# Scores and exponentials of layer 0 in two tiles of two heads; one TensorE allowance split into two; the norms behind layer 1 as threads of their own

## The chip, the core and the metric

The kernel is one program on one core of a Trainium2 chip. TensorE multiplies matrices from SBUF into PSUM, VectorE and ScalarE do elementwise work and evictions, GpSimd does some elementwise work and issues software DMAs, SyncE issues the other DMAs. All arithmetic is float32. The metric is the device time of one execution in microseconds (us); the kernel before is given by the median of 13 runs, and one further execution was profiled.

## The reference

The input x is 8 images of 256 channels by 32 x 32 positions. Two layers follow each other:

```python
# layer 0
x = x + L0_conv(_gn(x))          # 8 heads of 32 channels, 1024 queries,
                                 # 1426 keys: k and v maps pooled to 32^2, 16^2, 11^2, 5^2,
                                 # each with a 3x3 depthwise convolution and a layer norm
    # attn = softmax(q k^T * 32**-0.5);  out = attn v;  a 32x32 mix of each head;  projection
# layer 1, tokens t = [8, 1024, 256]
t = t + attention(_ln_t(t))      # one head of 256, softmax over 1024 keys, divided by its sum
t = t + ffn(_ln_t(t))            # 8 experts, three 256x256 matmuls each, relu between them;
                                 # the experts' outputs are weighed by a gate that is made
                                 # from the mean of all 8 images' normed tokens
```

So the feed-forward part needs the second norm (`_ln_t` behind layer 1's attention) of every image before its gate is known.

## The kernel before

`attention()` holds layer 0 and layer 1's attention of all images, `experts()` the feed-forward part. A third part, `layer0_general` and `layer1_general`, is run only for inputs for which the fast softmax could overflow; it is not run here and has no place in the profile.

**The main loop.** Layer 0's attention is 8 images x 2 groups of 4 heads x 2 halves of the queries (512 each) x 12 chunks of 128 keys (the last one has 18) = 384 steps. In step i, `scores` (L1434) issues four matmuls, one for each head, each on its own 32 rows of the array, into one PSUM tile `sc` of four banks, and ScalarE takes all of it through one exponential of 2048 columns into an SBUF tile `pt` (6 buffers). `sc` has one buffer, so the scores of step i+1 wait for the exponential of step i. Behind the scores of step i, TensorE has `values` of step i-1 (four matmuls, each on its own 32 columns of the array, into `pv`). Every second step, GpSimd issues a DMA that adds one `pt` tile onto the one before it (1 MB, written back to SBUF); VectorE adds such pairs up in `sums`, whose total is the softmax's denominator.

**What lies between the steps.** All other work is written as Python generators ("threads") with a rank: `unit` 0 (the sums and the division), `project` 1 (projection and residual, result to DRAM as `t1`), `keys_and_values` and `pool_levels` 2, `first_diagonals` 3, `prepare` 4 (the next image's group norm, maps and queries), `outputs` and the weights' set-up 5, `layer1` 6, `convolve` 7 (VectorE's convolution), `gates` 7. A thread yields what it needs next: an engine, the tiles that must be ready, a PSUM tag. `Flow` (L654) keeps a planned clock for each engine from fixed costs (0.00169 us a column for a TensorE matmul, a quarter and 0.05 us for one on 32 rows or columns), and `step()` resumes the first thread, in order of rank, that `runnable()` admits. The order of instructions on every engine is therefore fixed when the program is built.

**The allowance.** A TensorE piece is admitted while `credit` is above zero, or while the planned TensorE clock lies more than 0.5 us before the time at which `sc` will be free, less 0.5 us; its inputs have to be ready 1.5 us before that time in any case. Each step adds `PACE` = 3.2 us to `credit`, up to 1.5 times that; each piece takes its planned cost from it. All ranks share this one number.

**Layer 1.** `layer1` makes an image's scores in 16 pieces (tiles `p1`, 6 buffers), and stays at most six pieces ahead of `outputs`. `outputs` takes a quarter of an image's queries at a time: the sum of the exponentials, the product with v, the division into an SBUF tile `o`, bias and residual (`res`, read from `t1`), the store to `t2`, then `scale_tokens` (transposes on TensorE, statistics on VectorE, a power and a diagonal on GpSimd, a matmul that spreads the scale, a multiplication) and the store to `hn`. Only then does it take the next quarter. `o` and `res` have one buffer each.

**Behind the loop.** `experts()` runs the first two matmul stages of the experts (stage one with plain products, 4 x 512 columns) while layer 1 of the last image and the gate are still being finished (`PACE2` = 8 us of allowance a step). Once the gate is known, it goes on with seven products of 256 columns in place of eight.

Of the kernel before, what the change touches and what calls it, by code (L numbers as in the profile page):

```python
# [10 lines left out]
AF = mybir.ActivationFunctionType  # L11
ALU = mybir.AluOpType
# [4 lines left out]
P = 128  # L17
C = 256
HW = 1024
HEADS = 8  # L20
DH = 32
# [4 lines left out]
NE = 8  # L26
SCALE0 = DH ** -0.5
SCALE1 = C ** -0.5
PACE = 3.2
CAP = 1.5  # L30
NEVER = 1e9
MARGIN = 1.5
AHEAD = {"DVE": 4.0, "ACT": 2.0, "POOL": 4.0, "SP": 10.0}
# [2 lines left out]
PACE2 = 8.0  # L36
# [617 lines left out]
class Flow:  # L654
# [18 lines left out]
    def __init__(self, tc, kit):  # L673
        nc = tc.nc
        self.tc, self.kit = tc, kit
        self.now = dict.fromkeys(("PE", "DVE", "ACT", "POOL", "SP"), 0.0)
        self.last = {}
        self.ready, self.read, self.writer, self.reader, self.slots, self.open = {}, {}, {}, {}, {}, set()
        self.pe = self.Engine(self, "PE", nc.tensor)
        self.ve = self.Engine(self, "DVE", nc.vector)  # L680
        self.act = self.Engine(self, "ACT", nc.scalar)
        self.pool = self.Engine(self, "POOL", nc.gpsimd)
        self.sp = self.Engine(self, "SP", nc.sync)
        self.threads = []
        self.cut = {}
        self.also = {}
        self.credit, self.port = 0.0, 0.0

    def tile(self, pool, shape, tag, bufs=1):
        t = self.kit.tile(pool, shape, tag, bufs=bufs)  # L690
# [111 lines left out]
            self.threads.insert(at, thread)  # L802
        return thread

    def runnable(self, need):
        engine, tiles, tag = need
        if engine is None:
            return tiles()
        at = max([self.ready.get(n, 0.0) for t in tiles for n in self.keys(t)], default=0.0)
        pe = self.now["PE"]  # L810
        if engine == "PE":

            until = max(pe, self.free("sc") - 0.5)
            slot = self.free(tag) if tag is not None else 0.0
            return (
                not self.closed
                and (self.credit > 0 or pe < until - 0.5)
                and at + MARGIN <= until
                and slot <= until
            )  # L820

        now = self.now[engine]
        return now <= pe + AHEAD[engine] if at <= now + 0.3 else at <= pe + NEAR[engine]

    def resume(self, thread):
        pe = self.now["PE"]
        thread[1] = next(thread[0], None)
        if thread[1] is None:
            self.threads = [t for t in self.threads if t is not thread]
        self.credit -= self.now["PE"] - pe  # L830

    def step(self, pace=None):


        self.closed = pace is None
        if pace is not None:
            self.credit = min(self.credit + pace, CAP * pace)
        while True:
            thread = next((t for t in self.threads if self.runnable(t[1])), None)
            if thread is None:  # L840
                return
            self.resume(thread)

    def finish(self, done):

        while not done():
            self.credit, self.closed = 1.0, False
# [14 lines left out]
def attention(tc, kit, f, outer, ended, nb, consts, x, t1, t2, hn, bounds, vecs, q_t, kv_t, proj_t, gqk_t, wqk, wqkv, vecs1, w1_d, w1c, gate_d, wrc, vecs2, bnvec):  # L862
# [6 lines left out]
    with ExitStack() as ctx:  # L869
        l1, shared = outer  # L870
        wp = ctx.enter_context(tc.tile_pool(name="w0", bufs=1))
        work = ctx.enter_context(tc.tile_pool(name="work0", bufs=1))
        psum = ctx.enter_context(tc.tile_pool(name="psum0", bufs=1, space=PSUM))

        def T(pool, shape, tag, bufs=1):
            return f.tile(pool, shape, tag, bufs=bufs)
# [34 lines left out]
        heads = T(l1, [P, P + DH], "o")  # L911
        nc.scalar.dma_start(heads, consts[:, K_HEAD:K_SEL])
        head = heads[:, :P]

# [115 lines left out]
        ks, qs, vts = {}, {}, {}  # L1030
# [402 lines left out]

        def scores(b, c, sl, kc):  # L1434
            k0, w = KEY_CHUNKS[kc]
            t = T(psum, [P, 4, 512], "sc")
            for j in range(4):
                r = slice(DH * j, DH * j + DH)
                f.pe.matmul(t[:w, j, :], lhsT=ks[b, c][r, k0 : k0 + w], rhs=qs[b, c][r, sl], start=True, stop=True)
            pt = T(work, [P, 4, 512], "pt", bufs=6)  # L1440
            f.act.activation(pt[:w], t[:w], AF.Exp, scale=SCALE0)
            return pt

        def values(b, c, kc, pt, pv):
# [106 lines left out]
        projected, taken, written, probabilities = [0], [0], [0], []  # L1551
# [55 lines left out]
        def outputs():  # L1607

            for i in range(4 * nb):
                yield until(lambda: len(probabilities) > i)  # L1610
                b, q, p1, v = probabilities[i]
                res = T(l1, [P, 2, C], "res")
                f.sp.dma_start(res, t1[b][:, :, q])
                s = T(l1, [P, 2, C], "s")
                yield ve(*p1[:2])
# [15 lines left out]
                ps = small()  # L1631
                for m in range(2):
                    for kc in range(8):
                        if kc % 4 == 0 and (m or kc):
# [3 lines left out]
                            lhsT=v[:, kc, m * P : (m + 1) * P],  # L1638
                            rhs=p1[kc // 2][:, kc % 2, :],
                            start=kc == 0,  # L1640
                            stop=kc == 7,
                        )
                taken[0] += 1
                yield ve(ps, rec)
                o = T(l1, [P, 2, C], "o")
                f.ve.tensor_tensor(
                    o, ps.rearrange("p (m q) -> p m q", m=2), rec[:, None, :].to_broadcast([P, 2, C]), ALU.mult
                )
                for m in range(2):
                    f.ve.scalar_tensor_tensor(o[:, m, :], o[:, m, :], gb[:, m : m + 1], res[:, m, :], ALU.add, ALU.add)  # L1650
                f.sp.dma_start(t2[b][:, :, q], o)
                yield from scale_tokens(o, C)
                f.sp.dma_start(hn[b][:, :, q], o)
                written[0] += 1
                ended[0] = written[0] // 4

        def centred(cm, src, width, dst):

# [14 lines left out]
        def weights1():  # L1673
# [36 lines left out]
            ps = small()  # L1710
            for m in range(2):
                for k in range(2):
                    f.pe.matmul(
                        ps[:, m : m + 1],
                        lhsT=raw[:, k, C + m * P : C + (m + 1) * P],
                        rhs=bqkv[:, k : k + 1],
                        start=k == 0,
# [21 lines left out]
                f.ve.tensor_tensor(c, c, be_, ALU.add)  # L1739

            for e in range(NE):
                we = T(l1, [P, 2, C], "res")
                f.sp.dma_start(we, w1_d[:, e])
                yield act(we)
                wc = T(l1, [P, 2, C], "o")
# [33 lines left out]
        for i in range(len(steps) + 1):  # L1779
# [169 lines left out]
def experts(tc, kit, nb, t2, hn, h2d, w1c, w2_d, wo_d, bnvec, bo_d, gate_d, wrc, consts8, out, f, outer, ended, early):  # L1949
# [11 lines left out]
    with ExitStack() as ctx:  # L1961
# [152 lines left out]
        while not gated and n2 < NSTAGED:  # L2114
            first(n1)
            n1 += 1
            f.step(PACE2)
            if n1 > 1:
                for _ in second(n2, True):
                    pass  # L2120
                n2 += 1
                f.step(PACE2)
# [312 lines left out]
```

## Time and profile before

| | |
|---|---|
| median of 13 runs | 3499.58 us (3484.08 to 3506.56) |
| profiled execution | 3496.76 us, of which span 3495.0 us |
| granted TensorE clock, mean | 0.969 |
| busy | TensorE 92%, VectorE 65%, ScalarE 48%, GpSimd 14% |
| main loop (first to last scores matmul) | 102.6 to 2093.8 us |
| TensorE busy, 102 to 2094 us | 1799.3 of 1992 us |
| TensorE busy, 2420 to 3495 us | 1061.1 of 1075 us |

A busy share is a union of the instructions' spans; the granted clock is the share of TensorE's clock pulses that the chip let through. In the list of waits, the engine that waited stands first, then who ended its wait, then the sum, the number and the longest. In the groups of instructions, the columns behind the bar are the busy time, the mean duration of one instruction in ns, and the idle time of the engine just before them. A float32 matmul appears as two MATMUL instructions of one pass each, so the four matmuls of a step's scores are eight rows. Almost every instruction has line L667, a helper that records it, so the text goes by tiles.

### The profile page before, as it was taken

The page shows a single profiled execution, that of the slowest core. Times are in us where ns is not written, and L with a number is a line of the kernel's source. Part 1 is how long each engine was busy: PE and PEld are TensorE (multiplying, and loading weights), DVE is VectorE, ACT ScalarE, POOL GpSimd, SP SyncE. Part 2 cuts the span into 40 slices and gives each one's busy share as a digit, 9 for nine tenths or more (in the row PEclk, how much of TensorE's full clock was granted, in tenths as well). Part 3 has the DMA queues.
Part 4 walks back from the last instruction along what each step waited for, and adds up shares of the span by engine and source line. Part 5 has one row for each costly group of instructions (what it writes and reads, how often), then busy time and mean ns, then how long its engine had stood idle before and what let it go on. Part 6 is the DMA issues. An engine that isn't in the chain of part 4 may idle for free.

```text
span 3495.0 us, 39918 instructions
## 1 busy us (share of the span) xinstructions
PE 3227.9 (92%) x15276; PEld 1785.7 (51%) x15276; DVE 2277.6 (65%) x3922; ACT 1675.4 (48%) x2195; POOL 488.4 (14%) x616
## 2 busy tenths in 40 slices
PE   7787899899989989989999997998999999999998
PEld 3322244344424434433544354745777777777776
DVE  6686988778878787685554443314776566656665
ACT  3565666556566565555554542342223333333332
POOL 3122122131131221321121110004000000000000
PEclk9798999999999999999999999999999999999999
DMA  1356655644654564554556546223440000000000
GB/s 47 75 115 148 140 120 118 138 112 108 150 107 107 135 136 109 120 124 112 112 125 136 129 105 222 79 85 108 155 141 18 19 18 25 31 18 19 19 12 20
DMA packets 103880, 333.28 MB, mean 95 GB/s; under 512 B 12848, under 2 KB 38200, under 8 KB 80448
## 3 DMA queue, kind: packets, MB, share of 16 engines
q0 software_dynamic: 24576, 172.51, 25.2%
q1 hardware_dynamic: 75744, 156.16, 13.1%
q8 instruction: 122, 2.00, 0.2%
q10 hardware_dynamic: 3360, 1.97, 0.2%
q14 instruction: 78, 0.64, 0.1%
HBM read 96.23 MB, written 61.87 MB: 45 GB/s over the span
## 4 chain that ended last, share of the span: by engine, by line
PE 53%; DMA 3%; DVE 3%; ACT 2%; issue 1%; POOL 0%; SPq 0%; DVEq 0%; ACTq 0%; POOLq 0%
PE bank L667 24%; PE y L667 11%; PE sm L667 9%; PE sc L667 3%; PE sx L667 3%; PE pv L667 3%; ACT pt L667 2%; DMA pt<-pt 1%; DMA t<-xr 1%; DVE acc L667 1%; DVE rec L667 0%; DMA t<-t 0%; DMA xr<-in_x_dram 0%; DVE t L667 0%; DVE st L667 0%
## 5 line engine op out<-in xcount | busy, mean ns | idle before, releaser
L667 ACT ACTIVATE pt<-sc 128x2048 f32<-128x2048 f32 (+1 forms) x384 | 720.4, 1876 | 355.4 <-PE sc L667 260.0
L667 PE MATMUL sc<-q,kn 32*128 32x512 f32 (+1 forms) x3072 | 461.3, 671 | 135.2 <-ACT pt L667 134.2
L667 DVE SCALAR_TENSOR_TENSOR acc<-p,vec,acc 128x225 f32<-128x225 f32 (+7 forms) x928 | 521.3, 569 | 31.1 <-ACT acc L667 6.4
L667 PE MATMUL bank<-h,w2e 128*128 128x512 f32 x1024 | 478.4, 593 | 0.0
L667 ACT ACTIVATE h<-bank,bnvec 128x512 f32<-128x512 f32 x298 | 229.5, 770 | 475.5 <-PE bank L667 457.5
L667 DVE TENSOR_TENSOR pt<-pt,pt 128x1024 f32<-128x1024 f32 x320 | 382.5, 1238 | 107.3 <-DMA pt<-pt 102.6
L667 PE MATMUL pv<-pt,vt 128*32 128x512 f32 (+1 forms) x3072 | 426.9, 629 | 2.1 <-ACT att L667 2.1
L667 ACT ACTIVATE h<-c,bnvec 128x512 f32<-128x512 f32 x214 | 162.5, 807 | 321.6 <-DVE c L667 321.6
L667 POOL DMA_DIRECT2D pt<-pt x192 | 169.0, 880 | 990.1 <-ACT pt L667 862.5
L667 PEld LDWEIGHTS sc<-q,kn 32*128 32x128 f32 (+1 forms) x3072 | 119.6, 183 | 337.6 <-ACT pt L667 230.7
L667 DVE TENSOR_TENSOR c<-p1c,bank 128x512 f32<-128x512 f32 x107 | 73.5, 687 | 317.0 <-PE bank L667 317.0
L667 PEld LDWEIGHTS bank<-h,w2e 128*128 128x128 f32 x1024 | 193.7, 190 | 150.0 <-issue 138.2
L667 PEld LDWEIGHTS pv<-pt,vt 128*32 128x32 f32 (+1 forms) x3072 | 61.3, 109 | 316.0 <-issue 298.7
L667 POOL TENSOR_TENSOR rstd<-rstd,mhalf 128x4 f32<-128x4 f32 (+2 forms) x88 | 108.7, 1236 | 733.8 <-DVE rstd L667 600.2
L667 DVE TENSOR_TENSOR h<-h,gates 128x1024 f32<-128x1024 f32 x128 | 156.8, 1225 | 71.5 <-DMA h<-h 64.2
L667 PE MATMUL bank<-hn,w1e 128*128 128x256 f32 (+1 forms) x596 | 188.5, 445 | 10.3 <-DMA w2e<-in_w_dram 10.3
L667 PE MATMUL y<-t,s3e 128*128 128x256 f32 x768 | 188.0, 381 | 0.0
L667 PE MATMUL sm<-y,t 128*128 128x256 f32 x736 | 173.2, 383 | 0.0
L667 ACT ACTIVATE p<-sm 128x512 f32<-128x512 f32 (+1 forms) x151 | 88.2, 584 | 169.1 <-PE sm L667 142.9
L667 PEld LDWEIGHTS bank<-hn,w1e 128*128 128x128 f32 x596 | 113.5, 192 | 99.3 <-issue 91.8
L667 DVE RECIPROCAL rec<-rec 128x512 f32<-128x512 f32 x32 | 107.2, 3351 | 86.8 <-ACT rec L667 86.7
L667 PE MATMUL bank<-t,s1e 128*128 128x256 f32 x642 | 156.1, 379 | 1.7 <-DVE t L667 1.7
(291 smaller groups left out, 4672.5 us busy)
## 6 DMA issues: line engine op xcount, KB each, us to landing
pt<-pt POOLq DMA_DIRECT2D x160, 1024.0 KB, 7.4
h<-h SPq DMA_DIRECT2D x72, 512.0 KB, 4.1
xi<-in_x_dram SPq DMA_DIRECT2D x16, 512.0 KB, 7.1
t<-t SPq DMA_DIRECT2D x8, 1024.0 KB, 6.6
res<-t SPq DMA_DIRECT2D x32, 256.0 KB, 6.1
t<-o SPq DMA_DIRECT2D x32, 256.0 KB, 2.8
hn<-o SPq DMA_DIRECT2D x32, 256.0 KB, 5.6
hn<-hn SPq DMA_DIRECT2D x16, 512.0 KB, 5.5
```

Source lines behind the costliest of these rows:

```text
L667: ins = fn(*args, **kwargs)
```

## The change

1. `scores`: the tile `sc` becomes two tiles of two heads (two banks each, two buffers of the tag, so the same four banks). The four matmuls stay next to each other on TensorE, the first two into the first tile, the last two into the second; then two exponentials of 1024 columns follow, into the two halves of the same `pt` tile.
2. The allowance is split: ranks 0 to 4 have 4.0 us a step, ranks from 5 on 2.0 us, each up to 1.5 times that. The time up to which a piece may run is taken from the later of the two `sc` buffers.
3. `outputs` divides in place in PSUM, adds bias and residual into `res`, and starts the norm as a thread of its own (`norm`, rank 5, behind `outputs`). `o` is gone, `res` has two buffers, and a quarter may begin when the norm of the quarter before the last one has been issued.

The set-up tiles that used `o` now use `res`. The allowance of the loop in `experts()` is 8 us for either class.

```diff
-PACE = 3.2
-CAP = 1.5
+FILLER = 5
+PACE = 4.0
+PACE1 = 2.0
+CAP = (1.5, 1.5)
...
-    def runnable(self, need):
+    def runnable(self, need, rank=0):
...
-            until = max(pe, self.free("sc") - 0.5)
+            until = max(pe, max(map(self.end, self.slots.get("sc", [None]))) - 0.5)
...
-                and (self.credit > 0 or pe < until - 0.5)
+                and (self.credit[rank >= FILLER] > 0 or pe < until - 0.5)
...
-        self.credit -= self.now["PE"] - pe
+        self.credit[thread[2] >= FILLER] -= self.now["PE"] - pe
...
-            self.credit = min(self.credit + pace, CAP * pace)
+            for i in range(2):
+                self.credit[i] = min(self.credit[i] + pace[i], CAP[i] * pace[i])
...
         def scores(b, c, sl, kc):
             k0, w = KEY_CHUNKS[kc]
-            t = T(psum, [P, 4, 512], "sc")
-            for j in range(4):
-                r = slice(DH * j, DH * j + DH)
-                f.pe.matmul(t[:w, j, :], lhsT=ks[b, c][r, k0 : k0 + w], rhs=qs[b, c][r, sl], start=True, stop=True)
+            exps = []
             pt = T(work, [P, 4, 512], "pt", bufs=6)
-            f.act.activation(pt[:w], t[:w], AF.Exp, scale=SCALE0)
+            for u in range(0, 4, 2):
+                t = T(psum, [P, 2, 512], "sc", bufs=2)
+                for j in range(u, u + 2):
+                    r = slice(DH * j, DH * j + DH)
+                    f.pe.matmul(t[:w, j - u, :], lhsT=ks[b, c][r, k0 : k0 + w], rhs=qs[b, c][r, sl], start=True, stop=True)
+                exps.append((pt[:w, u : u + 2, :], t[:w]))
+            for out, t in exps:
+                f.act.activation(out, t, AF.Exp, scale=SCALE0)
             return pt
...
-                res = T(l1, [P, 2, C], "res")
+                yield until(lambda: scaled[0] >= i - 1)
+                res = T(l1, [P, 2, C], "res", bufs=2)
...
-                o = T(l1, [P, 2, C], "o")
-                f.ve.tensor_tensor(
-                    o, ps.rearrange("p (m q) -> p m q", m=2), rec[:, None, :].to_broadcast([P, 2, C]), ALU.mult
-                )
+                m2 = ps.rearrange("p (m q) -> p m q", m=2)
+                f.ve.tensor_tensor(m2, m2, rec[:, None, :].to_broadcast([P, 2, C]), ALU.mult)
                 for m in range(2):
-                    f.ve.scalar_tensor_tensor(o[:, m, :], o[:, m, :], gb[:, m : m + 1], res[:, m, :], ALU.add, ALU.add)
-                f.sp.dma_start(t2[b][:, :, q], o)
-                yield from scale_tokens(o, C)
-                f.sp.dma_start(hn[b][:, :, q], o)
-                written[0] += 1
-                ended[0] = written[0] // 4
+                    f.ve.scalar_tensor_tensor(res[:, m, :], m2[:, m, :], gb[:, m : m + 1], res[:, m, :], ALU.add, ALU.add)
+                f.sp.dma_start(t2[b][:, :, q], res)
+                f.spawn(norm(b, q, res), 5)
+
+        scaled = [0]
+
+        def norm(b, q, o):
+
+            yield from scale_tokens(o, C)
+            f.sp.dma_start(hn[b][:, :, q], o)
+            scaled[0] += 1
+            written[0] += 1
+            ended[0] = written[0] // 4
...
-                f.step(PACE)
+                f.step((PACE, PACE1))
```

More of the change, by code (lines that the diff above doesn't have):

```diff
@@ L686, in __init__ @@
         self.also = {}
-        self.credit, self.port = 0.0, 0.0
+        self.credit, self.port = [0.0, 0.0], 0.0
     def tile(self, pool, shape, tag, bufs=1):
@@ L836, in step @@
         if pace is not None:
-            self.credit = min(self.credit + pace, CAP * pace)
+            for i in range(2):
+                self.credit[i] = min(self.credit[i] + pace[i], CAP[i] * pace[i])
         while True:
-            thread = next((t for t in self.threads if self.runnable(t[1])), None)
+            thread = next((t for t in self.threads if self.runnable(t[1], t[2])), None)
             if thread is None:
@@ L846, in finish @@
         while not done():
-            self.credit, self.closed = 1.0, False
+            self.credit, self.closed = [1.0, 1.0], False
             thread = next((t for t in self.threads if t[1][0] is None and self.runnable(t[1])), None)
@@ L910, in attention @@
         ident, grp = kit.ident, con[:, K_GRP : K_GRP + P]
-        heads = T(l1, [P, P + DH], "o")
+        heads = T(l1, [P, P + DH], "res", bufs=2)
         nc.scalar.dma_start(heads, consts[:, K_HEAD:K_SEL])
@@ L1741, in weights1 @@
             for e in range(NE):
-                we = T(l1, [P, 2, C], "res")
+                we = T(l1, [P, 2, C], "res", bufs=2)
                 f.sp.dma_start(we, w1_d[:, e])
                 yield act(we)
-                wc = T(l1, [P, 2, C], "o")
+                wc = T(l1, [P, 2, C], "res", bufs=2)
                 yield from centred(cm, we, C, wc)
@@ L2116, in experts @@
             n1 += 1
-            f.step(PACE2)
+            f.step((PACE2, PACE2))
             if n1 > 1:
@@ L2121, in experts @@
                 n2 += 1
-                f.step(PACE2)
+                f.step((PACE2, PACE2))
         f.finish(lambda: gated)
```

## The prediction

> **What bounds the kernel now.** I read the slices first, then TensorE by stage, then the groups of one shape, then the waits, then the timeline of a stretch without filler.
>
> From the page, TensorE's busy share and granted clock in 40 slices:
>
> ```profile
> PE   7787899899989989989999997998999999999998
> PEclk9798999999999999999999999999999999999999
> ```
>
> Behind slice 27 TensorE is full at full clock, so no time is to be had there. What can move lies in the main loop. The loop by image (start:end, length, busy us of PE, PEld, DVE, ACT, POOL with counts, clock, DMA share, GB/s):
>
> ```profile
> 102.00:350.00 248.00, 196.72 (x1099) 74.94 (x1098) 175.60 (x364) 149.63 (x175) 50.47 (x61) 0.87 0.54 120
> 350.00:582.00 232.00, 209.15 (x1192) 85.83 (x1194) 192.32 (x336) 153.56 (x188) 54.35 (x64) 0.99 0.58 127
> 582.00:842.00 260.00, 237.32 (x1307) 108.66 (x1300) 204.62 (x366) 154.71 (x192) 58.60 (x68) 0.97 0.53 118
> 842.00:1090.00 248.00, 223.24 (x1235) 94.86 (x1235) 205.83 (x366) 153.51 (x186) 56.13 (x69) 0.96 0.56 125
> 1090.00:1339.00 249.00, 230.95 (x1308) 106.32 (x1306) 206.56 (x370) 152.56 (x187) 56.05 (x68) 0.99 0.56 127
> 1339.00:1602.00 263.00, 238.78 (x1289) 106.74 (x1288) 194.46 (x354) 151.18 (x185) 58.43 (x68) 0.94 0.53 119
> 1602.00:1858.00 256.00, 240.70 (x1359) 118.26 (x1358) 141.10 (x244) 147.34 (x175) 38.89 (x43) 0.97 0.53 117
> 1858.00:2094.00 236.00, 222.42 (x1285) 109.85 (x1288) 114.23 (x154) 119.97 (x123) 32.19 (x39) 0.99 0.57 124
> sum 1992.00, PE 1799.28 PEld 805.47 DVE 1434.72 ACT 1182.46 POOL 405.11; mean PE 224.91 PEld 100.68 DVE 179.34 ACT 147.81 POOL 50.64
> ```
>
> TensorE bounds every image, but idles 1992.0 - 1799.3 = 192.7 us of the loop, 51 of them in image 0, where no layer 1 exists yet. The missing clock, each length times (1 - clock), sums to 81 us. VectorE is at 71 to 83% through image 5, ScalarE at 59% of the loop.
>
> The scores and their exponential, shapes kept apart, then an eviction of 512 columns:
>
> ```profile
> L667 ACT ACTIVATE pt<-sc 128x2048 f32<-128x2048 f32 x352 | 660.8, 1877 | 327.6 <-PE sc L667 236.1 <-DMA pt<-pt 59.5 <-issue 14.2
> L667 PE MATMUL sc<-q,kn 32*128 32x512 f32 x2816 | 426.9, 677 | 127.7 <-ACT pt L667 126.6
> L667 ACT ACTIVATE att<-pv 128x512 f32<-128x512 f32 x32 | 18.9, 592 | 0.4 <-PE pv L667 0.4
> ```
>
> The waits:
>
> ```profile
> PE sc L667 <- ACT pt L667: 134.2, 98, 7.5
> ACT pt L667 <- DMA pt<-pt: 59.5, 17, 7.5
> PE sm L667 <- DVE xr L667: 23.6, 6, 5.9
> ```
>
> Of the idle 192.7 us, 134.2 are scores that wait for the exponential of the step before. Counted in the timeline, the 98 waits fall into 46 of 0.9 to 1.2 us (47.5 us together), 28 shorter ones (12.0) and 24 longer ones (74.6). The first kind is this, TensorE's timeline (start, length, group, idle before):
>
> ```profile
> 1957.05 1.07 PE L667 MATMUL pv<-pt,vt 128*32 128x512 f32 x8
> 1959.11 1.14 PE L667 MATMUL sc<-q,kn 32*128 32x512 f32 x8 [1.00 <-ACT pt L667]
> 1960.18 1.06 PE L667 MATMUL pv<-pt,vt 128*32 128x512 f32 x8
> 1962.25 1.14 PE L667 MATMUL sc<-q,kn 32*128 32x512 f32 x8 [1.00 <-ACT pt L667]
> ```
>
> A step without filler is scores 1.07, exponential 1.88 and handovers 0.19: 3.14 us, with 1.00 idle behind the values. The longer waits have another cause: the exponential itself started late, mostly because its `pt` buffer was still held by the adding DMA (59.5 us of ScalarE's waits) or because ScalarE had other work in front.
>
> **The split of the scores.** From 592 ns at 512 columns to 1877 at 2048, ScalarE's slope is 0.837 ns a column; 1024 columns take 1.02 us, two of them 2.04, so a step's exponentials end 0.16 later than now. Put the end of a step's scores at 0. The exponentials run 0.07 to 1.09 and to 2.11. Values fill TensorE to 1.07. The next first pair starts at about 1.15 and ends at 2.1, but the second pair has to wait until 2.2 and ends at 3.15, where the four end now (3.14): four heads next to each other ran at once, two and two run one after the other, and the idle 1.0 is filled with work that was not on the path before. Only the exponential gets ahead: its first half can start at 2.2 and both halves are done by 4.25, so if the next step is bare too, its scores start at 4.2 and end near 5.3 in place of 6.28. So one lone wait gains nothing and loses 0.16; of two waits in a row, the second gains 0.95. The 98 waits form 36 single ones, 18 runs of two, 2 of three and 5 of four: 18 + 2 + 10 = 30 pairs, 28 us. The other 68 waits lose 0.16 each, 11 us. Of the gain I keep half, because bare steps run into the ring of `pt`: a tile is held for two steps, GpSimd's issue (0.88), the DMA (7.4 to its landing) and two adds of 1.24, and one of six buffers is the running sum. Five buffers carry steps of x us only if 5x >= 2x + 10.8, x = 3.6; bare steps are under that already, and 17 waits for that DMA show it. Sum: 11 - 14 = -3 us, between -17 and +11.
>
> ScalarE's extra 384 x 0.16 = 61 us lie beside TensorE (59% busy, 62% after); without that cover they cost all 61. Where the exponential queues behind other ScalarE work the extra shows: I take +3, of 0 to 15. That the second pair carries a wait of its own, and the second matmul a signal, no row prices; the eight MATMULs of one step's scores start 7 ns apart within a pass, so I take 0, of 0 to 20 (0.05 a step). By the Trainium skill (TensorE: Matmul & The Clock Gate, The cost: per-tile semaphore tail), each further increment costs some 26 ns, an estimate of 10 us over 384 steps; no run here shows it.
>
> **The allowances and the norm threads.** In the planner's own costs, an image's ranks 0 to 4 come to 47 us of TensorE (maps 19, transposes 9, queries 7, projection 7, sums 4), 0.97 a step over 48 steps; layer 1 (scores 28, products with v 28, v 7, y 7, norms and sums 9: 79) to 1.64. Before, 3.2 served both, and layer 1 took what was left, in bursts; then it ran dry (from 970 to 1027 us nearly no layer 1 ran, and TensorE idled 1.16 us in each of 12 steps). With 2.0 of its own, layer 1 is stretched over at least 39 of 48 steps. `outputs` no longer waits for transposes, GpSimd's power (0.97) and diagonal (0.80) and a spreading matmul before it takes the next quarter, which keeps `p1` flowing. What this can win is the waits for want of filler once layer 1 exists. From 515 us on there are 61 waits of 73.7 us; less 14 long ones (38 us), 35 us remain. I take 20, of +10 (the pieces come at worse moments) to -45. No work is removed: where a stretch gets less layer 1, it goes behind the loop, where experts' products fill TensorE anyway. There the last image's norms overlap, the gate comes earlier, and each expert stage one done with seven products instead of eight saves about a fifth of 3.7 us: -3.
>
> The moved DMAs: `res` is loaded a quarter earlier, and with two buffers its issue on SyncE can wait for the store of `hn` two quarters back (5.6 us to landing), with image loads queued behind it; 32 times, nearly always long done: 0. The division into PSUM keeps its 0.69 us; VectorE writing PSUM has no row, 32 x 0.1 either way lies off the path.
>
> **The clock.** Image 7 has 13 waits for scores, most of about 1.0 us, and clock 0.99; image 5, with one of 6.2 and several of 2 us, has 0.94. The long waits throttle, not the bare steps, and nothing here shortens them. I take -8 of the 81 us, of 0 to -30. The Trainium skill (TensorE: Matmul & The Clock Gate, Part 1: The HAM clock gate) says that about 3.4 us of idleness halve the clock; so it speaks against counting the closed 1 us gaps as a gain in clock, and by the rule alone this term would be 0.
>
> Sum: -3 + 3 + 0 - 20 - 3 - 8 = -31 us on the profiled execution of 3496.8; the median lies 2.8 above, so 3469.
>
> **The rivals.**
>
> *Every lack of filler closes.* The 35 us, the full 28 us of pairs, 30 of clock, and some 12 of the long waits: -105, 3395. For it: two allowances of 6.0 in all against a need of 2.6. Against it: image 0 and most of image 1, with 37 of the waits (60.5 us), have no layer 1 to take from.
>
> *Nothing measurable.* The gain of the pairs goes to the ring, layer 1's gain is half: within 7 us, 0.2%, which is about what a measurement of this kernel can tell from no change.
>
> *The ring of `pt` decides (slower).* Up to 9 planned us of pieces between some steps and 2.65 us between others make the DMAs come in bunches. Place: ScalarE in front of an exponential. The point is 3.6 us a step, below which the bare runs are. Now 17 + 4 exponentials are held by the DMA or the adds behind it, 55 us late in all, and 38 of that reach TensorE. Doubled: +38, and 15 of clock, less the 20 of filler: +33, about 3533.
>
> *The pairs never run at once (slower).* If the wait between them makes the second pair follow the first in full steps too, one pass more stands on the path, 0.45 (the spacing of the values' passes) x 384 = 173 us, less the pairs' gain: about 3645. It decides if a full step's scores last over 1.07. Against it: a wait already satisfied does not hold TensorE in the rows of now; matmuls with one start without a gap.
>
> **How the numbers follow.** Forecast 0.46, own range 3440 to 3490. All filler 0.12, nothing 0.13, ring 0.19, pairs 0.10. Faster by over 0.2%: 0.46 + 0.12 = 0.58; same 0.13; slower 0.19 + 0.10 = 0.29. The range 3405 to 3545 leaves out the pairs' case and about half each of the strongest gain and a little of the ring's.
>
> **What would show it.** Right: runs of bare steps near 2.65 us a step, lone waits still there; `pt` exponentials of 1.02 us; full steps with 1.07 from scores to values; layer 1 in every 12 steps from 515 us on; the idle of the loop near 160 us. Wrong: more than 25 waits of ScalarE for the adding DMA, scores at 1.5 us in full steps, or a loop that ends earlier with the time given back behind it.

## The result and the profile after

The changed kernel took 3507.4 us (median of 11 runs, 3502.9 to 3513.4) beside 3497.6 us of the kernel before: a ratio of 1.0031, 95% interval [1.0019, 1.0043]. It is slower by 0.3%. The forecast was 3469 us, faster by 0.9%. The profiled execution took 3507.5 us, with a span of 3505.7 us and a clock of 0.964 (before 0.969).

TensorE in 40 slices, busy share and granted clock:

```profile
PE   7688999999989988999999989999999999999998
PEclk9698999999989989999999999999999999999999
```

A slice is 87.6 us. Counted from 0, slices 4 to 22 (the loop behind image 0) are mostly full now, but for three: 11, 14 and 15, from 964 to 1052 and from 1227 to 1402 us; in 11 and 14 the clock is lower as well. The loop by image (start:end, length, busy us of PE, PEld, DVE, ACT, POOL, clock, DMA share, GB/s):

```profile
101.00:354.00 253.00, 211.11 (x1071) 79.78 (x1069) 166.99 (x341) 146.79 (x209) 51.23 (x58) 0.84 0.52 114
354.00:569.00 215.00, 206.22 (x1114) 78.50 (x1110) 169.72 (x297) 145.95 (x214) 48.58 (x60) 0.96 0.60 132
569.00:817.00 248.00, 238.08 (x1282) 106.09 (x1280) 198.98 (x366) 159.90 (x242) 58.26 (x69) 0.97 0.57 128
817.00:1077.00 260.00, 241.54 (x1256) 106.08 (x1254) 206.64 (x342) 150.04 (x226) 56.24 (x68) 0.95 0.54 123
1077.00:1345.00 268.00, 243.01 (x1268) 108.40 (x1267) 186.91 (x339) 150.01 (x224) 55.23 (x66) 0.92 0.50 112
1345.00:1596.00 251.00, 245.12 (x1328) 113.00 (x1327) 212.28 (x366) 168.76 (x263) 53.95 (x68) 0.99 0.55 124
1596.00:1826.00 230.00, 224.01 (x1260) 101.60 (x1259) 170.97 (x308) 147.56 (x221) 40.28 (x46) 0.98 0.55 120
1826.00:2035.00 209.00, 203.86 (x1170) 91.02 (x1166) 102.90 (x132) 117.83 (x157) 33.81 (x35) 0.99 0.64 139
sum 1934.00, PE 1812.95 PEld 784.48 DVE 1415.39 ACT 1186.84 POOL 397.57; mean PE 226.62 PEld 98.06 DVE 176.92 ACT 148.36 POOL 49.70
```

TensorE now idles 1934.0 - 1812.95 = 121 us in the loop, where it idled 193, and the loop is 57.5 us shorter (1933.8 against 1991.3, first to last scores). Images 3 and 4 became longer, 260 and 268 against 248 and 249, and image 4 has the lowest clock behind image 0. What follows the loop grew by 69.4 us. The same columns from the loop's end to the end, before and then after:

```profile
2094.00:3495.00 1401.00, 1359.26 (x5030) 945.24 (x5022) 777.46 (x1221) 453.91 (x708) 49.79 (x80) 0.99 0.18 62
```

```profile
2035.00:3506.00 1471.00, 1433.88 (x5322) 998.88 (x5320) 795.88 (x1261) 470.96 (x741) 60.26 (x89) 0.99 0.20 70
```

So the loop ended earlier and the time was given back behind it, with TensorE full at full clock. Summed over the trace by tile, TensorE's time in the loop divides like this (us; an instruction counts for what it adds behind the one before it; layer 1 with its norms, sums and the set-up of its weights):

| | before | after |
|---|---|---|
| scores | 442.1 | 524.2 |
| idle | 192.7 | 121.0 |
| scores and idle together | 634.8 | 645.2 |
| layer 1 | 598.1 | 533.0 |
| all other | 758.3 | 755.7 |
| loop | 1991.3 | 1933.8 |

65.1 us of layer 1 went out of the loop. Counted in the same way behind it, layer 1 grew by 71.7 us there. 27 items of the experts' first stage were done with plain products instead of 21 (216 rows of 512 columns against 168), which put 20.5 us of plain rows in the place of 18.2: 2.3 us. The idle behind the loop fell by 4.9 (30.5 to 25.7), and the rest changed by 0.3: 69.4 us in all. So moving layer 1 is nearly neutral (71.7 in, 65.1 out, 4.9 less idle); what counts is the third line. The idle that was filled came back as longer scores, plus 10 us.

The exponentials, the scores and the waits (columns as in the lines of before):

```profile
L669 ACT ACTIVATE pt<-sc 128x1024 f32<-128x1024 f32 x704 | 682.6, 1023 | 336.6 <-PE sc L669 190.8 <-DMA pt<-pt 83.6 <-DVE pt L669 32.9
L669 PE MATMUL sc<-q,kn 32*128 32x512 f32 x2816 | 501.9, 678 | 63.1 <-ACT pt L669 60.1 <-ACT kn L669 1.0
```

```profile
PE sc L669 <- ACT pt L669: 75.1, 43, 7.7
ACT pt L669 <- DMA pt<-pt: 83.6, 25, 8.1
ACT pt L669 <- DVE pt L669: 34.6, 11, 5.5
```

The last of these was, before:

```profile
ACT pt L667 <- DVE pt L667: 12.8, 4, 4.3
```

The mean of one matmul is the same (678 against 677 ns); their union grew by 75 us, because in many steps the second pair now runs alone, behind a wait. Waits of the scores fell from 98 to 43, while ScalarE's waits for the adding DMA and the adds behind it rose from 72 (59.5 + 12.8) to 118 us (83.6 + 34.6).

The worst stretch is the end of image 4, here cut from the timeline (start, length, group, idle before; "..." stands for other rows):

```profile
1299.74 1.94 ACT L669 ACTIVATE pt<-sc 128x1024 f32<-128x1024 f32 x2 [5.52 <-DMA pt<-pt]
...
1300.81 2.04 PE L669 MATMUL sc<-q,kn 32*128 32x512 f32 x8 [0.76 <-ACT pt L669]
...
1302.79 1.07 PE L669 MATMUL pv<-pt,vt 128*32 128x512 f32 x8
...
1307.32 2.99 PE L669 MATMUL sc<-q,kn 32*128 32x512 f32 x8 [3.46 <-ACT pt L669]
...
1310.24 1.94 PE L669 MATMUL pv<-pt,vt 128*32 128x512 f32 x8
...
1319.83 1.94 ACT L669 ACTIVATE pt<-sc 128x1024 f32<-128x1024 f32 x2 [8.09 <-DMA pt<-pt]
...
1320.91 3.00 PE L669 MATMUL sc<-q,kn 32*128 32x512 f32 x8 [5.36 <-ACT pt L669]
```

There is little but scores and values on TensorE. Of image 4's last 12 steps, 6 have nothing else behind their scores in the trace (3 before), and of image 3's, 9 (1 before). Layer 1 had 0.14 us a step at the end of image 4 (2.08 before). In both kernels layer 1 of three images is done when these 12 steps begin (384 rows each of its scores and of its products with v). Before, the next image's pieces followed at once (32 rows of its v and 48 of its scores within the 12 steps); now none came. The steps run until no `pt` buffer is free; ScalarE waits 5 to 8 us, TensorE behind it, and the clock falls. This stretch (1275 to 1345 us) and the last 12 steps of image 3, in the columns of the loop's table:

```profile
1003.00:1077.00 74.00, 62.40 (x276) 23.57 (x274) 57.80 (x81) 36.10 (x50) 29.82 (x34) 0.84 0.48 100
1275.00:1345.00 70.00, 51.56 (x232) 14.87 (x233) 33.30 (x62) 29.28 (x37) 22.48 (x32) 0.78 0.42 86
```

The same 24 steps before took 64 and 61 us at clock 1.00:

```profile
1027.00:1091.00 64.00, 62.63 (x336) 29.47 (x340) 59.06 (x86) 42.62 (x54) 6.30 (x10) 1.00 0.48 95
1278.00:1339.00 61.00, 56.12 (x312) 25.39 (x312) 58.36 (x85) 34.82 (x36) 12.70 (x14) 1.00 0.53 112
```

### The profile page after: what moved, and what is told of

Its sections match the earlier page's. It is cut to its first block, busy times and chain, and to the rows that moved or that the text cites. A ratio compares the mean times of both kernels' runs of the same rounds, so it can differ in the third digit from the quotient of the medians.

```text
span 3505.7 us, 40279 instructions
## 1 busy us (share of the span) xinstructions
PE 3315.9 (95%) x15240; PEld 1818.4 (52%) x15240; DVE 2276.8 (65%) x3895; ACT 1697.1 (48%) x2573; POOL 491.3 (14%) x616
## 4 chain that ended last, share of the span: by engine, by line
PE 73%; DMA 6%; DVE 5%; ACT 2%; issue 2%; POOL 1%; SPq 0%; ACTq 0%; DVEq 0%; POOLq 0%
PE bank L669 24%; PE sm L669 17%; PE y L669 11%; PE sc L669 9%; PE pv L669 6%; PE sx L669 6%; DMA pt<-pt 3%; DVE acc L669 1%; ACT pt L669 1%; DVE pt L669 1%; DMA xr<-in_x_dram 1%; DMA t<-xr 1%; DMA hn<-pool 1%; DVE rec L669 1%; POOL pool L669 0%
## 5 line engine op out<-in xcount | busy, mean ns | idle before, releaser
L669 ACT ACTIVATE pt<-sc 128x1024 f32<-128x1024 f32 (+1 forms) x768 | 743.9, 1021 | 366.8 <-PE sc L669 216.4
L669 PE MATMUL sc<-q,kn 32*128 32x512 f32 (+1 forms) x3072 | 547.1, 676 | 78.5 <-ACT pt L669 75.1
L669 DVE SCALAR_TENSOR_TENSOR acc<-p,vec,acc 128x225 f32<-128x225 f32 (+7 forms) x928 | 543.1, 591 | 30.7 <-ACT acc L669 6.0
L669 ACT ACTIVATE h<-bank,bnvec 128x512 f32<-128x512 f32 x310 | 239.1, 771 | 486.3 <-PE bank L669 468.3
L669 PEld LDWEIGHTS sc<-q,kn 32*128 32x128 f32 (+1 forms) x3072 | 154.1, 184 | 323.3 <-ACT pt L669 219.0
L669 ACT ACTIVATE h<-c,bnvec 128x512 f32<-128x512 f32 x202 | 153.4, 807 | 307.1 <-DVE c L669 307.1
L669 DVE TENSOR_TENSOR c<-p1c,bank 128x512 f32<-128x512 f32 x101 | 69.4, 687 | 296.3 <-PE bank L669 296.2
L669 PE MATMUL bank<-hn,w1e 128*128 128x256 f32 (+1 forms) x620 | 203.9, 459 | 10.3 <-DMA hn<-hn 10.3
L669 PE MATMUL sm<-y,t 128*128 128x256 f32 x776 | 183.6, 384 | 0.4 <-DVE xr L669 0.4
L669 PE MATMUL sm<-p,v 128*128 128x256 f32 x736 | 170.5, 385 | 3.6 <-DVE xr L669 1.9
L669 PEld LDWEIGHTS sm<-y,t 128*128 128x128 f32 x776 | 143.3, 190 | 51.4 <-issue 27.1
```

The lines of the kernel that those rows point to most:

```text
L669: ins = fn(*args, **kwargs)
```

## The experiments

All ratios are against the kernel before, with 95% intervals; 1% is 35 us.

**First: the chip or the order.** The split acts twice. On the chip it lets the first pair start earlier. In the planner (`Flow`), the same two tiles change the planned times and so the order of all other pieces. Theory A: the split only turns idle time into a second pair that runs alone. B: the split is good or harmless on the chip, and the new order costs. C: the ring of `pt` is what costs.

*The split in the order of before.* Two tiles and two exponentials on the chip; the planner keeps one tile, and the two exponentials together have the price of the one. Nothing else of the change.

```diff
+            if ins and self.key(ins[0]).startswith("sc_"):
+                return 0.1 + 0.00087 * n
...
+            ts = [kit.tile(psum, [P, 2, 512], "sc", bufs=2) for _ in range(2)]
...
+            slot = f.slots.setdefault("sc", [None])
+            f.ready[ts[0].name] = f.end(slot[0])
+            slot[0] = ts[0].name
+            f.alias[ts[1].name] = ts[0].name
```

> Two tiles and two exponentials, every other instruction in the order of the kernel before. Theory A (the split only turns idle time into a second pair of scores that runs alone): scores busy in the loop rises from 442 to about 510-530 us, idle falls from 193 to about 110-130, their sum stays at 630-645, time within 8 us of before. Theory B (the split frees TensorE, and the loss of the change comes from the new order): sum of the two falls by 25 or more, time 20 to 40 us under before. Theory C (the later end of the exponentials makes the pt ring worse): more than 22 waits of ScalarE for the adding DMA, time 10 to 25 us over before.

Measured: 3493.9 us, 0.9988 [0.9976, 1.0001]. The trace shows the trade that the prediction described: idle in the loop 192.7 to 115.9 us, scores 442.1 to 506.2; together 634.8 to 622.1. That lies between the marks of A (630 to 645) and B (a fall of 25 or more), and the gain of 20 to 40 us that B named is not there. Its waits:

```profile
PE sc L667 <- ACT pt L667: 57.9, 38, 7.0
ACT pt L667 <- DMA pt<-pt: 71.2, 22, 7.7
```

*Two exponentials of one whole tile, order of before.*

```diff
+            for u in range(2):
+                f.act.activation(pt[:w, 2 * u : 2 * u + 2, :], t[:w, 2 * u : 2 * u + 2, :], AF.Exp, scale=SCALE0)
```

> One tile of four heads as before, but two exponentials of 1024 columns on it, order of the kernel before. It has the longer exponential without the earlier release. All theories: 0.16 us for each wait of the scores, 98 waits, so +10 to +20 us over before. Theory A: slower than the split in the order of before by at most 5 us beyond what pairs of bare steps gain, so by 5 to 25. Theory B: slower than it by 40 or more. Theory C: the waits for the adding DMA rise here as well.

Measured: 3495.4 us, 0.9992 [0.9978, 1.0006]. The expected loss is not there. Two exponentials in a row take 1.94 us (the timeline above), not 2.04, so a step's end is 0.06 us later and not 0.16.

*The order of after with the whole tile.* The planner sees the two tiles of the change; the chip gets one tile of four banks and one exponential. All else is as in the changed kernel.

```diff
+            t = kit.tile(psum, [P, 4, 512], "sc", bufs=1)
...
+            names = [f"{t.name}_{u}" for u in range(2)]
+            ins = nc.scalar.activation(pt[:w], t[:w], AF.Exp, scale=SCALE0)
```

> The order of the changed kernel, its allowances and norm threads, but one tile of four heads and one exponential. Theory A: time within 12 us of the changed kernel, scores busy back at 440 us, idle up to 190-205. Theory B: 25 us or more slower than the changed kernel. Theory C: faster than the changed kernel by 8 to 20 us, with fewer than 20 waits for the adding DMA.

Measured: 3523.5 us, 1.0070 [1.0049, 1.0090]. Undoing the split on the chip alone repairs nothing: the changed kernel is faster than this one. That is against A, though by 16 us only, between the 12 that A allowed and the 25 that B asked for; and C needs no split on the chip to appear (82.8 us of waits for the adding DMA here too). B is left in its weaker form: the split is harmless on the chip, and the new order costs. The experiments below test that.

**Second: which part.** The diff was taken apart. P: the allowances cost. S: the split costs, through the planner's clock.

*Norm threads alone* (part 3 of the change on the kernel before), *and with the allowances* (parts 2 and 3, whole tile, planned as such; this is its edit against the changed kernel).

```diff
+            t = T(psum, [P, 4, 512], "sc")
...
-            for u in range(0, 4, 2):
-                t = T(psum, [P, 2, 512], "sc", bufs=2)
...
+            f.act.activation(pt[:w], t[:w], AF.Exp, scale=SCALE0)
```

> The kernel before with the norms behind layer 1 as threads and two res buffers, one allowance of 3.2, one tile of four heads. If the norm threads keep layer 1 supplied: 10 to 20 us under before, idle in the loop 165-180. If they do nothing by themselves: within 7 us. If they hurt (VectorE's division in PSUM holds the PSUM slot longer): 5 to 15 us over before.

> Norm threads and the split allowance, one tile of four heads, order as the planner makes it. Counted in the order of TensorE's instructions, 57 steps have no filler (65 before, 59 with the norm threads alone, 85 in the changed kernel). Theory P (the split allowance costs the time: the changed kernel in its own order but with whole tiles took 3523, the norm threads alone 3464): about 3500 to 3520. Theory S (the split of the scores costs it through the planner's clock: a step without filler is planned at 2.4 us in place of 3.3, so more steps pass before other work is ready): 3455 to 3475.

Measured: 3463.6 us, 0.9911 [0.9890, 0.9931], and 3458.5 us, 0.9897 [0.9878, 0.9917]. The norm threads are worth 31 us, the allowances nothing that can be told from none. The changed kernel's order on whole tiles had taken 1.0070: the same chip parts as the second of these, 1.7% apart by the order alone.

*The split alone* (part 1), *split and norm threads* (parts 1 and 3), and these *two in the order of the norm threads alone* (the planner told as in the first experiment).

> Only the split of the scores on the kernel before, planner left free; 84 steps without filler. Theory P: like the split in the order of before, 3485 to 3500. Theory S: 3505 to 3525, with scores and idle together at 645 us or more, against 622 in the order of before.

> Norm threads and the split of the scores, one allowance of 3.2, planner left free; 65 steps without filler. Theory P: 3450 to 3465, as nothing of the allowance is in it. Theory S by its count of empty steps: 3465 to 3490, above the norm threads alone.

> Norm threads, and the split of the scores in exactly the order of the kernel with the norm threads alone (59 empty steps), so that the planner's clock does not see the split. The split was worth 6 us in the order of before: both theories 3450 to 3464; if it beats the norm threads alone by 2 to 12 us it is the best version here.

Measured: 3510.0 us, 1.0044 [1.0030, 1.0059]; 3503.4 us, 1.0020 [1.0003, 1.0036]; 3467.7 us, 0.9927 [0.9904, 0.9949]. The second lies above both expectations. The last two have the same parts on the chip and differ in the order alone: 0.9%. In the loop, scores and idle take 633 us in the one and 594 in the other.

**Third: all parts on the chip, other planned prices.** S as above; H: two tiles cost something on the chip once norms and allowances are there.

*The changed kernel with the planner told of a whole tile* (parts 2 and 3 free, part 1 as in the first experiment).

> All three parts of the change on the chip (two tiles, two exponentials, the split allowance, norm threads), but the planner's clock sees one tile and one exponential of 2048, so the order is that of the run with whole tiles (3458.5). If the cost sits in the planner's clock (theory S): 3450 to 3470. If the two tiles cost it on the chip once the order is otherwise the new one (theory H): 3485 to 3510.

Measured: 3463.7 us, 0.9899 [0.9879, 0.9919], the same as without the split (0.9897), 44 us under the changed kernel. Its image ends 3 and 4 are filled again:

```profile
1022.00:1090.00 68.00, 67.26 (x344) 31.80 (x340) 54.73 (x82) 42.55 (x66) 5.98 (x10) 0.99 0.46 98
1275.00:1333.00 58.00, 55.25 (x281) 21.79 (x281) 50.69 (x69) 33.72 (x45) 11.05 (x14) 0.94 0.60 122
```

*No split at all, only the planner's price of the exponential changed*, 1.98 to 1.0 and to 2.3 (the chip's takes 1.88 in each):

```diff
+            if ins and self.key(ins[0]).startswith("sc_"):
+                return 1.0
...
```

> No split on the chip: one tile, one exponential, as in the run that took 3458.5. Only a number of the planner is changed: the exponential of 2048 is planned at 1.0 us instead of 1.98, so that a step without filler is planned at 2.4 us, as the changed kernel plans it; planned loop 1749 us (changed kernel 1747, run with whole tiles 1826). Theory S: 3490 to 3525, empty steps 84 against 57, scores and idle together 635 to 660. Theory H: 3450 to 3470.

> Whole tiles with norm threads and the split allowance, the exponential planned at 2.3 us instead of 1.98: no planned step is under 3.6 us, the rate at which the ring of pt can be kept up by my estimate. Theory S, carried on in its own direction: at or under the run with whole tiles, 3440 to 3460, with fewer waits of ScalarE for the adding DMA (16 there). If the plan was right already: within 5 us of 3458.5.

Measured: 3540.0 us, 1.0109 [1.0090, 1.0128], and 3450.3 us, 0.9864 [0.9842, 0.9886]. The first is 15 us above what S expected. One number that the chip never sees is worth 90 us. Waits of the short plan; then, in the columns of the loop's table, the end of its image 4, the changed kernel's bad stretch once more:

```profile
PE sc L669 <- ACT pt L669: 173.1, 123, 7.4
```

```profile
1288.00:1353.00 65.00, 42.54 (x224) 9.78 (x228) 32.84 (x50) 27.39 (x23) 21.89 (x29) 0.74 0.50 104
```

*The changed kernel with each exponential planned at 1.57 us* instead of 1.09.

> The changed kernel with one number of the planner raised: each exponential of 1024 columns planned at 1.57 us instead of 1.09, so a run of steps without filler is planned near 3.2 us. Theory S: 3455 to 3485. Theory H: 3500 to 3515.

Measured: 3520.2 us, 1.0063 [1.0044, 1.0083]: a miss. Score waits fell to 26, 37.4 us, but TensorE then waited for other things; of its idle 146.5 us in the loop, 109 are not waits for the exponential (46 in the changed kernel).

**Fourth: a law or a draw.** After that miss it was open whether any new order is a draw with a spread of tens of us (N), or the time follows the planned step (S), or tiles that come free one by one spoil the plan (H2).

*No split, exponential planned at 1.5 and at 1.9 us; the changed kernel at 1.3 each; the split in the order of the 2.3 us plan.* The edits are the price line and the first experiment's.

> Norm threads and split allowance on whole tiles, exponential of a step planned at 1.5 us (the chip's takes 1.88; 1.98 planned gave 3459 us, 1.0 gave 3540, 2.3 gave 3450). If the time goes with how far the planner's clock runs ahead of the chip (S), this lies between its neighbours: 3490 to 3520. If any change of a planned cost only deals the same pieces out anew, with a better or a worse hand each time (N), it can fall anywhere from 3450 to 3530, with no order among 1.0, 1.5, 1.9, 1.98 and 2.3.

> The same with the exponential planned at 1.9 us, 4% below 1.98. S: 3455 to 3470, next to 3459. N: the spread that a small change makes by itself, up to 30 us either way: 3430 to 3490. How far it lies from 3459 is the measure of what a new order is worth with hardly any change in the plan's length.

> The changed kernel with each of the two exponentials of a step planned at 1.3 us (1.09 gave 3507 us, 1.57 gave 3520; the chip takes 1.02). S, if 1.57 was too long as well: a value near 3465 to 3490 between the two. N: 3480 to 3530, as the two neighbours. If two tiles that come free one by one in the plan are bad for the order whatever they cost (H2): 3500 to 3525.

> All three parts on the chip (two tiles, two exponentials), in the order that whole tiles with an exponential planned at 2.3 us give: the order of the kernel that took 3450 us. If the split itself is worth nothing on the chip, 3445 to 3460; if the lone second pairs cost, 3460 to 3475; if the pairs' gain shows now that few long waits are left, 3430 to 3445.

Measured: 3503.5 us, 1.0006 [0.9992, 1.0019]; 3473.9 us, 0.9920 [0.9902, 0.9939]; 3500.4 us, 0.9995 [0.9982, 1.0008]; 3444.8 us, 0.9839 [0.9819, 0.9859], the fastest of all, with these waits:

```profile
PE sc L669 <- ACT pt L669: 49.4, 31, 6.3
ACT pt L669 <- DMA pt<-pt: 48.9, 19, 6.4
```

*The changed kernel, a scores matmul planned at twice its price on TensorE* (so that a lone pair has 1.07 us), *and with its two tiles planned to come free together.*

```diff
+            if self.key(out).startswith("sc_"):
+                return c / 2 + 0.1
```

```diff
+        if tag == "sc":
+            self.ready[t.name] = max(map(self.end, slots))
```

> The changed kernel, with only the planner's price of a scores matmul on TensorE doubled: each pair is planned at 1.07 us, so a planned step without other work lasts 3.2 us of TensorE as on the chip, while ScalarE keeps 1.09 for each exponential and the two tiles still come free one by one. If the length of the planned bare step is what spoils the order (S): 3450 to 3480. If tiles that come free one by one are bad whatever they cost (H2): 3495 to 3525.

> The changed kernel, with only one line of the planner changed: both tiles of a step are planned to be free when the later of the two before them is (they still are two tiles with two exponentials, planned at 1.09 us each). Both S and H2 expect 3445 to 3475, for the planned bare step becomes 3.4 us and nothing comes free one by one. If it stays above 3490, neither is the cause, and the two tiles do harm in the order in some other way.

Measured: 3569.5 us, 1.0202 [1.0188, 1.0216], and 3495.4 us, 0.9987 [0.9976, 0.9997]. Both misses; by the second's own mark (above 3490), neither S nor H2 would be the cause. But that expectation had the planned step wrong: the planner lets the second pair run beside the first exponential, so the step is 0.15 + 0.53 + 0.15 + 2.18 = 3.0 us, not 3.4.

The series side by side. A planned bare step of a whole tile is four matmuls (1.07), two handovers of 0.15 and the exponential; with two tiles that come free one by one, the values and the pairs overlap the exponentials, and it comes to 2.3 us in the changed kernel. "Empty" is the number of the 384 steps whose scores have nothing behind them but values in TensorE's order.

| planned | bare step, us | empty | us | ratio |
|---|---|---|---|---|
| whole, 1.0 | 2.4 | 89 | 3540.0 | 1.0109 |
| whole, 1.5 | 2.9 | 73 | 3503.5 | 1.0006 |
| whole, 1.9 | 3.3 | 69 | 3473.9 | 0.9920 |
| whole, 1.98 | 3.35 | 57 | 3458.5 | 0.9897 |
| whole, 2.3 | 3.7 | 55 | 3450.3 | 0.9864 |
| two together, 1.09 each | 3.0 | 75 | 3495.4 | 0.9987 |
| two, 1.09 each (the change) | 2.3 | 85 | 3507.4 | 1.0031 |
| two, 1.3 each | 2.6 | 67 | 3500.4 | 0.9995 |
| two, 1.57 each | 3.1 | 72 | 3520.2 | 1.0063 |
| two, pairs doubled | 3.2 | 62 | 3569.5 | 1.0202 |

For whole tiles the time follows the planned step in order over five values; a mere draw would give this order once in 120 times (N is unlikely). It follows unevenly: 0.08 us of price from 1.9 to 1.98 is worth 15 us, 0.32 from 1.98 to 2.3 is worth 8. Two tiles planned to come free together fit into that series (3.0 us lies between 2.9 and 3.3). Two tiles one by one do not: no price brought them under 3500. That their release is the reason is consistent with this, but released together they gained only 0.4% over the changed kernel, so it is not shown. Open is what spoils these orders at longer prices. In the one with doubled pairs the waits for want of the exponential are few, and others stand out:

```profile
PE sc L669 <- ACT pt L669: 57.1, 35, 7.4
PE sm L669 <- DVE res L669: 24.2, 12, 4.1
```

A planner whose TensorE is slower than the chip's believes inputs to be ready that are not; that reading was not tested by itself.

What goes with the time in all these orders, the two misses included, is scores and idle together: over the traces of the 20 kernels their sum and the span have a correlation of 0.95, from 589 us at 3444 (the fastest) and 605 at 3448 (no split) over 645 at 3506 (the change) to 671 at 3540 (planned at 1.0) and 664 at 3561 (pairs doubled). They are part of the span, so this says where the time sits and not why.

## Why the prediction was wrong

**The step that failed.** The part on the split prices it as an event on the chip, and leaves the order of everything else where it was. But `step()` and `runnable()` read the planned end of `sc`, and the planner was given a bare step of 2.3 us instead of 3.35. The chip needs more: in the trace, the bare steps took 3.5 us on average, and those right behind another bare one 4.0. In the planner's clock more steps pass before the same inputs are ready, so more are left bare (85 empty ones against 65), and at the ends of images 3 and 4 there is little left to fill with. By the ratios, the split seen by the planner costs 1.0031 - 0.9899 = 1.3%, 46 us, where the sum had none. The order as the cause is shown three times over: by the order of after without the split (1.0070), by the changed kernel's parts in another order (0.9899), and by the short plan without any split (1.0109). That the short planned step is what makes the order bad is shown for whole tiles alone. For two tiles that come free one by one, longer prices left fewer steps empty (62 to 72) and did not bring the time back, so that what else is wrong with their orders stays open.

**The split on the chip: -3, right.** With the order held, five pairs of kernels give -0.12% (against before), +0.16% (norm threads), +0.02% (norms and allowances), -0.25% (the 2.3 us plan) and -0.39% (the order of the change, with 85 empty steps): -4, +6, +1, -9 and -14 us, all within the -17 to +11 of the prediction. The mechanism (idle turned into a second pair alone) is in the table of the loop. The term of 0.16 us a step was mis-sized; it is 0.06, and ScalarE's busy time rose by (682.6 + 61.3) - (660.8 + 59.6) = 23.5 us instead of 61. For the waits and signals of the pairs 0 was taken, of 0 to 20; the estimate of 10 us from the Trainium skill (TensorE: Matmul & The Clock Gate, The cost: per-tile semaphore tail) does not show in these five differences, whose mean is -4 us, though a gain of the pairs could hide it.

**Allowances and norms: -20, too small.** Together they gave -36 us (0.9897), the norm threads alone -31, the allowances no more than the noise. The reason given for the threads (the next quarter no longer waits for the norm) fits a loop with 35 us less of scores and idle (634.8 to 599.9), and waits for the adding DMA down from 59.5 to 41.5 us. Layer 1 stretched over at least 39 of 48 steps did not come true: 9 of the last 12 steps of image 3 and 6 of those of image 4 had nothing but values behind the scores.

**Clock: -8, wrong sign.** Length times (1 - clock) sums to 100 us after, 81 before. In the split with the order of before, idle fell by 77 us and the mean clock did not rise (0.965 against 0.969), so closing gaps of 1 us gained no clock. The rule of the Trainium skill (TensorE: Matmul & The Clock Gate, Part 1: The HAM clock gate) that some 3.4 us of idleness halve the clock was the better guide. This trace agrees with it in part. Behind an idle 0.76 us (1300.81 above) the values took 1.07 us; behind 3.46 us they took 1.94, with a granted clock of 0.50. But an idle 1.86 us was enough as well, again with a clock of 0.50:

```profile
1293.36 2.99 PE L669 MATMUL sc<-q,kn 32*128 32x512 f32 x8 [1.86 <-ACT pt L669]
1296.28 1.94 PE L669 MATMUL pv<-pt,vt 128*32 128x512 f32 x8
```

So one idle stretch of 3.4 us is not needed here; what decides is not shown.

**The tail.** Layer 1 behind the loop was nearly neutral, as said (65.1 us out, 71.7 in, 4.9 less idle), but instead of stage-one items saved (-3), six more were done with plain products. The term was mis-sized too: the six cost 2.3 us, 0.4 each, a tenth of the 3.7 and not a fifth.

**The rivals.** That the pairs never run at once is refuted: in 224 of the 302 steps with other work behind them the values still start about 1.07 us behind the scores (298 of 320 before). In 55 it is more than 1.6 us; 20 of these stand at cut clock (18 of 19 before), and in the other 35 the second pair comes late, so that it runs alone in full steps, too. Of the marks named in advance, the exponentials are 1.02 us long, bare steps behind bare ones took 4.0 us and not 2.65, and the idle of the loop fell even further than the 160 us expected, to 121, with no gain in time. The ring of `pt` had the right sign: its waits rose from 72 to 118 us, with 25 waits for the DMA, just at the bound named. But it is a consequence: with the same chip parts in the order of a whole tile, the same waits are 74.5 us and the loss is gone. The last sentence of the prediction, "a loop that ends earlier with the time given back behind it", is what the profile shows.

## What to carry to other kernels

Where a planner fixes the order of instructions, an edit to a tile or a buffer count is also an edit to the plan: first look at what planned time it changes and whether that time is as long as the chip's, and measure the edit once in the old order and the old parts once in the new order. Idle time that is filled with work that was not needed there before is no gain; add up the idle and the work that replaces it (here scores and idle together) before believing a fuller engine. When several parts come in one change, price and run each alone: here -31 us of one part were hidden under +46 of another.

## What the hardware showed beyond that

Four matmuls on 32 rows of the array run at once in 1.07 us; after a wait between the pairs, the same four take 2.04 us (1300.81 above), as two pairs one after the other (the second starts 0.92 us behind the first). With the clock cut to 0.50 they take 3.00. Two exponentials of 1024 columns in a row cost 0.06 us more than one of 2048 (1.94 against 1.88), and dividing in place in PSUM took 698 ns where the division into SBUF took 690 (before, then after):

```profile
L667 DVE TENSOR_TENSOR o<-sm,rec 128x512 f32<-128x512 f32 x20 | 13.8, 690 | 40.7 <-PE sm L667 40.7
L669 DVE TENSOR_TENSOR sm<-sm,rec 128x512 f32<-128x512 f32 x23 | 16.0, 698 | 59.5 <-PE sm L669 59.5
```
